# A convolution and attention stack in one loop of slots: another order of the prologue, and other slots for the work behind the loop

## The chip, the cores and the metric

The kernel runs on one core of a Trainium2 chip. The metric is the device time of one execution in microseconds (us). Engines are named as the profile names them: PE is TensorE (PEld its weight loads), DVE is VectorE, ACT is ScalarE, POOL is GpSimd, and SP is SyncE, which issues the DMAs here.

## The reference

The input is x, eight images of 128 channels and 36 x 36 points, all in float32. Two layers are applied, each added to its input.

```python
# layer 0: group norm, 1x1 convolution, attention of all 1296 points over the 34x34 inner ones
x = _conv(_gn(x), w_x) + b_x
q = _conv(x, w_qx, 'SAME'); k = _conv(x, w_kx, 'VALID'); v = _conv(x, w_vx, 'VALID')
a_x = v @ softmax(q^T k)            # the same for a constant image c, which becomes a bias
h = tanh(_conv(concat([x, a_x]), w_h) + b_h)
x = x + _conv(h, w_o) + b_o
# layer 1, on tokens t (8 x 1296 x 128): additive attention, then experts
q = LN(t) @ Wq^T + bq;  k = LN(t) @ Wk^T + bk
scores = sum_d w[d] * tanh(q[i, d] + k[j, d])
t = t + softmax(scores) @ LN(t)
t = t + experts(LN(t))              # 64 experts, each takes its 8 best tokens of an image
```

The scores of layer 1 need a tanh for each pair of points and each of 128 channels. The kernel writes them as a sum of quotients: "features" of queries and keys are exponentials of sums with signs, products of features give a numerator n and a denominator d for groups of terms, and the score is the sum of n / d.

## The kernel before, in words

**Units and slots.** For an image (batch b of 8), the 1296 queries are cut into 3 chunks of 432 and the keys into ten tiles of 128 and a remainder of 16. A chunk with a key tile is a unit; a unit with a full tile has 12 slots, one with the remainder 2, so there are 8 x 3 x (120 + 2) = 2928 slots. `SLOTS` says which rows of which feature block a slot k uses: for k = 0, 1 mod 3 two groups of 32 rows, for k = 2 mod 3 two groups of 64 rows.

**A slot.** `numerators(p)` issues on PE the two products n of slot p (each 432 columns, a PSUM bank each), `denominators(p + 3)` the two products d of the slot three later (`LAG`), followed on ACT by the Ln of both (L898) and, every second slot, one Exp over four (L901), which gives 1 / d. `terms(p)` on DVE multiplies n by 1 / d. In most slots these are two multiplications into rp (L929), which POOL adds up (L936, L938). In the slots of `DVE_PAIRS` = (2, 5, 8, 11) DVE multiplies and adds by itself, four operations (L918 to L925). `sums(u)` joins both totals on POOL, `exps` takes the Exp of the score on ACT (L958).

**Banks.** n products and all background matmuls take their PSUM banks in turn from one pool of four (`ps_n`); d has a pool of two pairs (`ps_d`).

**Work behind the loop.** All other work of layer 0 and layer 1 is written as generators, which are advanced between slots: `normal` (group norm and the 1x1 convolution), `conv_keys`, `layer0`, `tokens`, `keys`, `query_block`, `attend`, `gating`. They stand in four lanes: `first_of_all`, `urgent`, `gates`, `background`. A step says whether the next one has matmuls and how many slots it must rest. Steps without matmuls, most of them emptying a PSUM bank by DVE or ACT, run in `take_turns` ahead of a slot's products; steps with matmuls run in `matmul_turn` behind them, at most one a slot. `balance` allows background matmuls `PACE` columns a slot. `bmm` counts the columns. While the loop works on batch b, the lanes prepare batch b + 1; on the last batch there is none to prepare. Every engine runs its own queue in order, so this order of emission is the order on each engine.

**Convolutions.** A 3x3 convolution works on sums and differences of neighbouring columns (`xwin`, L371 to L375) with "turned" taps: `load_taps` loads three parts of the weight, forms half sums (L308 to L311) on DVE and stores the result in DRAM for later batches. `conv_turns` does four turns of three matmuls each (tile pc) for every group of rows.

**The prologue** is batch 0's share, done before the loop in program order: loads on SP; a matmul chain that makes the constant image's bias hb out of wvc (L218 to L227); `normal(0)`, with statistics at L327; the sign matrix, built on POOL (`signs`, L505); `conv_keys(0)`; `features` (L520 to L552), which multiplies the attention weights by the signs; `layer0(0)`, whose values' and queries' taps are loaded and turned at its start; `tokens(0)`; `keys(0)` for the first three tiles, which are stored in DRAM (kd) and read back (kf) by `prefetch`; three query blocks; and the first three `denominators`.

**After the loop** come the gates of the last batch, the experts and the output.

Of the kernel before, what the change touches and what calls it, by code (L numbers as in the profile page):

```python
# [2 lines left out]

# [41 lines left out]
NF = 8  # L45
# [13 lines left out]
PACE = 365  # L59
# [10 lines left out]
def kernel(  # L70
# [55 lines left out]
    with ExitStack() as loop, ExitStack() as score:  # L126
# [37 lines left out]

        load_x(0)
        wx_s = loaded(w_x, "w_x")
        bx_s = loaded(b_x, "b_x")
        wh_s = loaded(w_h, "w_h")
# [4 lines left out]
        gw_s = loaded(gate_w, "gate_w")  # L173
        gb_s = loaded(gate_b, "gate_b")
# [4 lines left out]
        nc.sync.dma_start(bw_s, bw.to_broadcast([128, 1]))  # L179
        neg_half = const.tile([128, NT], F32, tag="neg_half", name="neg_half")  # L180
# [33 lines left out]

        wvc_s = big_tile("wvc_s")[:, : 9 * C]
        nc.sync.dma_start(wvc_s, w_vc.rearrange("i t o -> i (t o)"))  # L218
        pv = aux("pv")
        for t in range(9):  # L220
            mm(pv[:, :1], wvc_s[:, t * C : (t + 1) * C], c0_s, start=(t == 0), stop=(t == 8))
        vc = small.tile([C, 1], F32, tag="vc", name="vc")
        nc.vector.tensor_copy(vc, pv[:, :1])
        ph = aux("ph")
        mm(ph[:, :1], wh_s[:, 2, :], vc, start=True, stop=True)
        hb = const.tile([C, 1], F32, tag="hb", name="hb")
        nc.vector.tensor_add(hb, ph[:, :1], bh_s)  # L227
# [65 lines left out]
        turned_taps = {}  # L293

        def load_taps(w, name):

            t = big_tile(name)[:, : 12 * C]
            h = t.rearrange("p (y j c) -> p y j c", y=3, j=4)
            if name in turned_taps:
                nc.sync.dma_start(t, turned_taps[name])  # L300
                return h
            g = w.rearrange("i (y x) o -> i y x o", x=3)
            g1 = chunk_tile("g1")[:, : 3 * C].rearrange("p (y c) -> p y c", y=3)
            nc.sync.dma_start(h[:, :, 0, :], g[:, :, 0, :])
            nc.sync.dma_start(h[:, :, 3, :], g[:, :, 2, :])
            nc.sync.dma_start(g1, g[:, :, 1, :])
            half = chunk_tile("half")[:, : 3 * C].rearrange("p (y c) -> p y c", y=3)
            nc.vector.tensor_add(half, h[:, :, 0, :], h[:, :, 3, :])  # L308
            nc.vector.tensor_scalar(half, half, 0.5, None, ALU.mult)
            nc.vector.scalar_tensor_tensor(h[:, :, 1, :], g1, 0.5, half, ALU.mult, ALU.add)  # L310
            nc.vector.scalar_tensor_tensor(h[:, :, 2, :], g1, -0.5, half, ALU.mult, ALU.add)  # L311
            turned_taps[name] = dram.tile([C, 12 * C], F32, tag=name, name=f"{name}_d")
            nc.sync.dma_start(turned_taps[name], t)
            return h
# [3 lines left out]
        def normal(b):  # L318

            if b not in xs:  # L320
                load_x(b)
            r = xs[b][:, :N]
            taps["k"] = load_taps(w_k, "wk_t")
            yield step(4)
            st = small.tile([C, NCH, 6], F32, tag="gn_st", name="gn_st")
            for c in range(NCH):
                nc.vector.bn_stats(st[:, c, :], r[:, c * CH : (c + 1) * CH])  # L327
                yield step()
            mv = small.tile([C, 2], F32, tag="gn_mv", name="gn_mv")
            nc.vector.bn_aggr(mv, st)  # L330
            yield matmuls(1)
            pm = aux("pm")
            bmm(pm[:, :1], gavg, mv[:, 0:1], start=True, stop=True)
            yield TAKE
            gm = small.tile([C, 1], F32, tag="gm", name="gm")
            nc.vector.tensor_copy(gm, pm[:, :1])
            dev = small.tile([C, 1], F32, tag="dev", name="dev")
            nc.vector.tensor_sub(dev, mv[:, 0:1], gm)
            nc.vector.scalar_tensor_tensor(dev, dev, dev, mv[:, 1:2], ALU.mult, ALU.add)
            yield matmuls(1)  # L340
            pv = aux("pgv")
            bmm(pv[:, :1], gavg, dev, start=True, stop=True)
            yield TAKE
            ve = plus_eps(pv[:, :1], 1e-5, [C, 1])
            yield step(2)

            rs = small.tile([C, 1], F32, tag="gn_rs", name="gn_rs")
            rsqrt(rs, ve)
            wxn = chunk_tile("wxn")[:, :C]
            nc.gpsimd.tensor_scalar(wxn, wx_s, rs, None, ALU.mult)  # L350
            yield matmuls(3)
            pb = aux("pb")
            bmm(pb[:, :1], wxn, gm, start=True, stop=True)
            yield TAKE
            bxn = small.tile([C, 1], F32, tag="bxn", name="bxn")
            nc.vector.tensor_sub(bxn, bx_s, pb[:, :1])
            yield matmuls(1)
            for c in range(NCH):
                px = aux("px")
                bmm(px[:, :CH], wxn, r[:, c * CH : (c + 1) * CH], start=True, stop=True)  # L360
                yield TAKE
                nc.vector.tensor_scalar(
                    xpad[:, 1 + c * RC : 1 + (c + 1) * RC, 1 : 1 + W],
                    px[:, :CH].rearrange("p (a b) -> p a b", b=W), bxn, None, ALU.add,
                )

                xe, xo = (xpad[:, 1 + c * RC : 1 + (c + 1) * RC, i::2] for i in range(2))
                u = xwin.rearrange("p j (a b) -> p j a b", b=HW)[:, :, 1 + c * RC : 1 + (c + 1) * RC]
                eng = nc.vector if b == 0 else nc.gpsimd
                e0, e1, o0, o1 = xe[:, :, :HW], xe[:, :, 1:], xo[:, :, :HW], xo[:, :, 1:]  # L370
                eng.tensor_sub(u[:, 0], e0, e1)  # L371
                eng.tensor_add(u[:, 1], o0, e1)
                yield step()
                eng.tensor_sub(u[:, 2], e1, o0)
                eng.tensor_sub(u[:, 3], o1, o0)  # L375
                yield matmuls(1)
# [6 lines left out]
        def conv_keys(b):  # L383
            k = convolved["k"] = big_tile("k0")
            for r0, nr in KROWS:
                yield from conv_turns(
                    taps["k"], (r0, nr), 1, grid(k[:, r0 * WV : (r0 + nr) * WV], WV), True
                )

        def layer0(b):  # L390
# [5 lines left out]
            wv_t = load_taps(w_v, "wv_t")  # L396
            v = big_tile("v0")
            wq_t = load_taps(w_q, "wq_t")
# [112 lines left out]

        def features(sign):
# [4 lines left out]
            feat = []  # L517
            for name, wt in (("a_q", wq1), ("a_k", wk1)):
                wt_s = chunk_tile("w_in")[:, :C]
                nc.sync.dma_start(wt_s, wt)  # L520
                tp = aux("w_t")
                nc.tensor.transpose(tp[:, :C], wt_s, ident)
                wT = chunk_tile("wT")[:, :C]
                nc.vector.tensor_copy(wT, tp[:, :C])
                a = const.tile([C, NF * 128], F32, tag=name, name=name)
                for o in range(0, NF * 128, 512):
                    pa = aux("pa")
                    mm(pa, wT, sign[:, o : o + 512], start=True, stop=True)
                    nc.vector.tensor_copy(a[:, o : o + 512], pa)
                feat.append(a)  # L530
            a_q, a_k = feat
# [3 lines left out]
            nc.vector.tensor_add(wb[:, 1:2], bq_s, bk_s)  # L535
            pcs = aux("pcs")
            for q in range(NF):
                mm(pcs[:, 2 * q : 2 * q + 2], sign[:, q * 128 : (q + 1) * 128], wb,
                   start=True, stop=True)
            cs_s = const.tile([128, NF], F32, tag="cs", name="cs_s")  # L540
# [7 lines left out]
            nc.vector.tensor_tensor(absw, absw, w1_s, ALU.max)  # L548
            psw = aux("psw")
            mm(psw[:, :1], ones, absw, start=True, stop=True)  # L550
            eb_s = const.tile([128, 1], F32, tag="eb", name="eb_s")
            nc.vector.tensor_sub(eb_s, bw_s, psw[:, :1])  # L552
            return a_q, a_k, cs_s, fb_s, eb_s
# [81 lines left out]
        def keys(b, tiles):  # L635
# [3 lines left out]
            for t in tiles:  # L639
                o, n = KT[t]  # L640
                for q0 in (0, NF // 2):
# [6 lines left out]
                    ks = kstp.tile([128, NF // 2, 128], F32, tag="ks", name="ks")  # L648
# [203 lines left out]
        def prefetch(u):  # L852
            if u < len(units):
# [140 lines left out]
        def take_turns(p):  # L994
            for lane in lanes:
                if lane.due(p, False):
                    lane.run(p)

        def matmul_turn(p):
# [3 lines left out]
            for lane in lanes:  # L1003
                while lane.due(p, True) and behind[0] == before:
                    if lane is not first_of_all and balance[0] < 0 or lane is gates and urgent:
                        break
                    lane.run(p)
            balance[0] = min(balance[0] - (behind[0] - before) + PACE, PACE)

        load_x(1)  # L1010
        drain(normal(0))
        sign = signs()
        drain(conv_keys(0))
        a_q, a_k, cs_s, fb_s, eb_s = features(sign)
        drain(layer0(0), tokens(0), keys(0, order[:3]))
# [5 lines left out]
        urgent.append(keys(0, order[3:]))  # L1021
        for u in range(2):
            prefetch(u)
        for p in range(LAG):
            denominators(p)
        pending = deque()
        for p, (u, k) in enumerate(slots):
# [12 lines left out]
            take_turns(p)  # L1040
# [13 lines left out]
            matmul_turn(p)  # L1054
# [6 lines left out]
        take_turns(len(slots))  # L1061
# [185 lines left out]
```

## Time and profile before

| What | us |
|---|---|
| median of 3 runs | 6183.36 (6181.84 to 6194.64) |
| the profiled execution | 6189.61 |
| its span, first to last instruction | 6187.9 |
| prologue, to the first multiplication of the loop | 189.8 |
| loop, to the last one | 5828 |
| after the loop | 170 |

Busy time in the span: PE 5946.4, ACT 5275.0, DVE 4799.7, POOL 4584.2 us. A busy PE is a modelled figure, since matmuls are pipelined. An fp32 matmul of the program appears as two MATMUL records. A wait is written "who <- for whom", with its total, how often and the longest one; a group line gives line, engine, operation, tiles, shapes, number, busy time, mean of one in ns, and the engine's idle time just ahead of it with what ended most of that.

### The profile page before, as it was taken

What the parts mean: (1) busy time and instruction counts of PE and PEld (TensorE: products, weight loads), DVE (VectorE), ACT (ScalarE), POOL (GpSimd) and SP (SyncE); (2) the same over time, 40 slices, a digit from 0 to 9 for tenths busy, and PEclk for the clock granted to TensorE, in tenths of its full rate; (3) what the DMA queues carried; (4) which work ended last, traced back from release to release, by engine and by line L of the source; (5) the groups of instructions that cost most, each with busy time, mean ns of one, the idle gap of its engine ahead of it and who ended that gap; (6) DMA issues with size and microseconds to landing.
All of it is one profiled execution on the core that took longest, in us unless ns stands there. A gap on an engine that the chain in (4) does not pass through costs nothing.

```text
span 6187.9 us, 93159 instructions
## 1 busy us (share of the span) xinstructions
PE 5946.4 (96%) x33576; PEld 2834.5 (46%) x33576; DVE 4799.7 (78%) x9525; ACT 5275.0 (85%) x5371; POOL 4584.2 (74%) x2794
## 2 busy tenths in 40 slices
PE   7999999999999999999999999999999999999996
PEld 5454444544544445444445444454444444544443
DVE  3687778877788787877887777887778878788872
ACT  1798998988989888889988899898998988999980
POOL 3677877777778777778777786877777777787870
PEclk9999999999999999999999999999999999999997
DMA  1210011000110002100111001110011000100017
GB/s 43 70 36 22 21 68 38 33 26 28 67 39 24 26 30 69 37 24 23 50 48 38 22 24 63 41 36 22 21 65 41 31 25 28 63 31 28 25 55 276
DMA packets 150383, 271.40 MB, mean 44 GB/s; under 512 B 45408, under 2 KB 74976, under 8 KB 149920
## 3 DMA queue, kind: packets, MB, share of 16 engines
q1 hardware_dynamic: 149920, 265.44, 12.8%
q8 instruction: 265, 4.34, 0.3%
q14 instruction: 198, 1.62, 0.1%
HBM read 200.94 MB, written 64.19 MB: 43 GB/s over the span
## 4 chain that ended last, share of the span: by engine, by line
PE 65%; DVE 11%; POOL 8%; ACT 8%; issue 8%; DMA 1%; SPq 0%; POOLq 0%; DVEq 0%; ACTq 0%
PE n L875 30%; PE d L875 10%; PE pa L258 7%; ACT lq L898 5%; PE pc L258 5%; DVE n L923 4%; POOL accp L938 4%; DVE rp L929 3%; PE s L258 3%; PE pk L258 3%; DVE accd L925 2%; POOL qf L673 1%; POOL accp L936 1%; PE d L880 1%; PE pq L258 1%
## 5 line engine op out<-in xcount | busy, mean ns | idle before, releaser
L938 POOL TENSOR_TENSOR accp<-accp,rp 128x864 f32<-128x864 f32 x1440 | 2915.1, 2024 | 996.5 <-DVE rp L929 943.5
L875 PE MATMUL n<-qf,kf 32*128 32x432 f32 (+1 forms) x11520 | 3283.6, 574 | 58.9 <-DVE accd L925 19.1
L898 ACT ACTIVATE lq<-d 128x864 f32<-128x864 f32 x2928 | 2517.6, 879 | 555.8 <-PE d L875 498.0
L875 PE MATMUL d<-qf,kf 32*128 32x432 f32 (+1 forms) x11520 | 2907.7, 563 | 46.4 <-ACT lq L898 40.5
L929 DVE TENSOR_TENSOR rp<-n,lq 128x432 f32<-128x432 f32 x3912 | 2160.8, 600 | 557.9 <-PE d L875 398.8
L901 ACT ACTIVATE lq<-lq 128x1728 f32<-128x1728 f32 (+1 forms) x1464 | 2398.2, 1638 | 46.3
L875 PEld LDWEIGHTS n<-qf,kf 32*128 32x128 f32 (+1 forms) x11520 | 1185.9, 185 | 1588.2 <-DVE rp L929 469.1
L875 PEld LDWEIGHTS d<-qf,kf 32*128 32x128 f32 (+1 forms) x11520 | 1046.9, 186 | 449.8 <-issue 241.7
L923 DVE TENSOR_TENSOR n<-n,lq 128x432 f32<-128x432 f32 x1440 | 812.0, 608 | 251.8 <-PE n L875 195.2
L925 DVE TENSOR_TENSOR accd<-n,accd 128x432 f32<-128x432 f32 x1440 | 868.1, 603 | 24.7
L936 POOL TENSOR_TENSOR accp<-rp 128x864 f32<-128x864 f32 x240 | 485.2, 2022 | 244.8 <-DVE rp L929 244.7
L673 POOL TENSOR_SCALAR qf<-qf,cs_s 128x432 f32<-128x432 f32 x192 | 260.7, 1364 | 47.0 <-ACT qf L672 47.0
L258 PEld LDWEIGHTS pa<-xh,e 128*108 128x108 f32 x1920 | 222.1, 174 | 142.9 <-DVE rp L929 63.3
L947 POOL TENSOR_TENSOR accd<-accp,accd 128x432 f32<-128x432 f32 x240 | 265.3, 1106 | 23.3 <-DVE accd L925 3.0
L258 PE MATMUL pa<-xh,e 128*108 128x129 f32 x1920 | 261.3, 283 | 19.9 <-DVE accd L925 13.9
L945 POOL TENSOR_TENSOR accp<-accp 128x432 f32<-128x432 f32 x240 | 264.7, 1103 | 15.8
L258 PE MATMUL s<-q,k 128*116 128x432 f32 x480 | 230.3, 568 | 4.2 <-DVE accd L925 2.7
L444 ACT ACTIVATE e<-s 116x432 f32<-116x432 f32 x240 | 124.8, 520 | 118.7 <-PE s L258 118.4
L258 PEld LDWEIGHTS pk<-xT,a_k 128*128 128x128 f32 x1408 | 171.6, 193 | 105.9 <-DVE n L923 31.8
L435 POOL TENSOR_TENSOR tot<-tot,e 116x432 f32<-116x432 f32 x192 | 212.1, 1105 | 7.3 <-ACT e L444 4.5
L918 DVE TENSOR_TENSOR accd<-n,lq 128x432 f32<-128x432 f32 x240 | 145.1, 604 | 86.7 <-PE n L875 49.7
L258 PE MATMUL pa<-e,vw 116*128 116x432 f32 x480 | 204.6, 549 | 0.0
(208 smaller groups left out, 3870.2 us busy)
## 6 DMA issues: line engine op xcount, KB each, us to landing
kf<-kd SPq DMA_DIRECT2D x240, 512.0 KB
kd<-ks SPq DMA_DIRECT2D x160, 256.0 KB
w<-in_weight_dram SPq DMA_DIRECT2D x32, 1024.0 KB
wk_t<-wk_t_d SPq DMA_DIRECT2D x7, 768.0 KB
wv_t<-wv_t_d SPq DMA_DIRECT2D x7, 768.0 KB
wq_t<-wq_t_d SPq DMA_DIRECT2D x7, 768.0 KB
x<-in_x_dram SPq DMA_DIRECT2D x8, 648.0 KB
t<-tokd SPq DMA_DIRECT2D x96, 54.0 KB
```

The lines of the kernel that those rows point to most:

```text
L258: mm(out, lhsT, rhs, **kw)
L673: nc.gpsimd.tensor_scalar(qf[:, 1, :], qf[:, 0, :], cs_s[:, q : q + 1], None, ALU.mult)
L875: mm(outs[h][:, :CH], kf[rows[h], q, :], qf_of[b, c, q][rows[h], part, :], start=True, stop=True)
L898: nc.scalar.activation(lq[:, o : o + n, :], d[:, :n, :CH], AF.Ln)
L901: nc.scalar.activation(some, some, AF.Exp, scale=-1.0)
L923: mult(ns[h], ns[h], lq[:, o + h, :])
L925: nc.vector.tensor_add(live["d"], ns[h], live["d"])
L929: mult(rp[:, h, :], n, lq[:, o + h, :])
L936: nc.gpsimd.tensor_add(live["p"], live["r"], rp)
L938: nc.gpsimd.tensor_add(live["p"], live["p"], rp)
L945: nc.gpsimd.tensor_add(s[:, 0, :], s[:, 0, :], s[:, 1, :])
L947: nc.gpsimd.tensor_add(d, s[:, 0, :], d)
```

## The change

Loads are issued in another order: x, the 1x1 weight, the raw taps of the keys' convolution, the attention weights, the raw taps of values and queries, then the rest; the load of the second image moves from the prologue to `normal(1)`. Turning the keys' taps moves behind the group norm's variance on DVE (five operations for four); those of values and queries are turned on POOL, ahead of the signs. The chain of the constant image (`context`) and the features become generators, one step of which is taken at each step of `layer0(0)` after the ninth. Before the first denominators only one key tile is computed, straight into its kf buffer; the next two follow the first denominators. In the loop, steps without matmuls are not run in the slots of `DVE_PAIRS`, and steps with matmuls not just ahead of them, save those of the first lane. `PACE` goes from 365 to 400 and the cap on saved columns from `PACE` to twice that.

```diff
-PACE = 365
+PACE = 400
...
+        def load_raw_taps(w, name):
+            h = big_tile(name)[:, : 12 * C].rearrange("p (y j c) -> p y j c", y=3, j=4)
+            g = w.rearrange("i (y x) o -> i y x o", x=3)
+            g1 = chunk_tile("g1")[:, : 3 * C].rearrange("p (y c) -> p y c", y=3)
+            nc.sync.dma_start(h[:, :, 0, :], g[:, :, 0, :])
+            nc.sync.dma_start(h[:, :, 3, :], g[:, :, 2, :])
+            nc.sync.dma_start(g1, g[:, :, 1, :])
+            raw_taps[name] = (h, g1)
+
         load_x(0)
         wx_s = loaded(w_x, "w_x")
         bx_s = loaded(b_x, "b_x")
+        load_raw_taps(w_k, "wk_t")
+        w_in = [loaded(w, "w_in", chunks, "chunk") for w in (wq1, wk1)]
+        load_raw_taps(w_v, "wv_t")
+        load_raw_taps(w_q, "wq_t")
...
+        def context():
+            wvc_s = big_tile("wvc_s")[:, : 9 * C]
+            nc.sync.dma_start(wvc_s, w_vc.rearrange("i t o -> i (t o)"))
+            yield
+            pv = aux("pv")
+            for t in range(9):
+                mm(pv[:, :1], wvc_s[:, t * C : (t + 1) * C], c0_s, start=(t == 0), stop=(t == 8))
+            yield
...
+        def turn_taps(name, eng):
+            h, g1 = raw_taps[name]
+            half = chunk_tile("half")[:, : 3 * C].rearrange("p (y c) -> p y c", y=3)
+            eng.tensor_add(half, h[:, :, 0, :], h[:, :, 3, :])
+            eng.tensor_scalar(half, half, 0.5, None, ALU.mult)
+            eng.tensor_scalar(g1, g1, 0.5, None, ALU.mult)
+            eng.tensor_add(h[:, :, 1, :], half, g1)
+            eng.tensor_sub(h[:, :, 2, :], half, g1)
+            turned_taps[name] = dram.tile([C, 12 * C], F32, tag=name, name=f"{name}_d")
+            nc.sync.dma_start(turned_taps[name], h.rearrange("p y j c -> p (y j c)"))
...
             ve = plus_eps(pv[:, :1], 1e-5, [C, 1])
+            if b == 0:
+                turn_taps("wk_t", nc.vector)
             yield step(2)
...
+                first = (b, t) == (0, order[0])
+                if first:
+                    kf_of[0] = kfp.tile([128, NF, 128], F32, tag="kf", name="kf")
...
-                    ks = kstp.tile([128, NF // 2, 128], F32, tag="ks", name="ks")
+                    if first:
+                        ks = kf_of[0][:, some, :]
+                    else:
+                        ks = kstp.tile([128, NF // 2, 128], F32, tag="ks", name="ks")
...
-        def take_turns(p):
+        def take_turns(p, k):
             for lane in lanes:
-                if lane.due(p, False):
+                if lane.due(p, False) and (k not in DVE_PAIRS or lane is first_of_all):
                     lane.run(p)
 
-        def matmul_turn(p):
+        def matmul_turn(p, k):
             before = behind[0]
             for lane in lanes:
                 while lane.due(p, True) and behind[0] == before:
-                    if lane is not first_of_all and balance[0] < 0 or lane is gates and urgent:
+                    paced = balance[0] < 0 or k + 1 in DVE_PAIRS
+                    if lane is not first_of_all and paced or lane is gates and urgent:
                         break
                     lane.run(p)
-            balance[0] = min(balance[0] - (behind[0] - before) + PACE, PACE)
+            balance[0] = min(balance[0] - (behind[0] - before) + PACE, 2 * PACE)
 
-        load_x(1)
         drain(normal(0))
+        for name in ("wv_t", "wq_t"):
+            turn_taps(name, nc.gpsimd)
         sign = signs()
         drain(conv_keys(0))
-        a_q, a_k, cs_s, fb_s, eb_s = features(sign)
-        drain(layer0(0), tokens(0), keys(0, order[:3]))
+
+        aside = chain(context(), features(sign))
+        for i, _ in enumerate(layer0(0)):
+            if i > 8:
+                next(aside, None)
+        drain(aside)
+        a_q, a_k, cs_s, fb_s, eb_s = (feat[n] for n in ("a_q", "a_k", "cs_s", "fb_s", "eb_s"))
+        drain(tokens(0), keys(0, order[:1]))
         for i, q in enumerate(IN_TURN):
...
-        urgent.append(keys(0, order[3:]))
-        for u in range(2):
-            prefetch(u)
         for p in range(LAG):
             denominators(p)
+        drain(keys(0, order[1:3]))
+        prefetch(1)
+        urgent.append(keys(0, order[3:]))
```

## The prediction, made before the result was known

> **What bounds the kernel.** I read the page first, then stretches of the span, then ScalarE's waits in the loop, then the prologue's timeline. The page's first line, and busy times in one batch in mid-loop against the last third of the last batch (columns: stretch, length, busy us of PE, PEld, DVE, ACT, POOL, granted clock, DMA share, GB/s):
>
> ```profile
> PE 5946.4 (96%) x33576; PEld 2834.5 (46%) x33576; DVE 4799.7 (78%) x9525; ACT 5275.0 (85%) x5371; POOL 4584.2 (74%) x2794
> ```
>
> ```profile
> 3150.00:3890.00 740.00, 723.27 (x4077) 343.85 (x4073) 594.04 (x1179) 656.01 (x668) 569.53 (x346) 0.98 0.11 37
> ...
> 5804.00:6018.00 214.00, 205.08 (x1131) 88.99 (x1126) 177.94 (x345) 198.21 (x190) 167.32 (x93) 0.99 0.07 21
> ```
>
> PE at 98% is modelled and includes time in which it waits with a matmul in its array. A real batch takes 740 us, 247 a chunk; a chunk of the last batch, with next to no work of another batch behind it, takes 214. ScalarE is the engine nearest its limit: 656 of 740, so 84 us idle a batch, 28 a chunk; in the last chunk 16. Next, what ScalarE waits for in the loop (190 to 6018 us; us in total, times, longest), what holds PE over the whole span, and two groups of VectorE's work in slots 2, 5, 8, 11:
>
> ```profile
> ACT lq L898 <- PE d L875: 493.0, 615, 3.3
> ```
>
> ```profile
> PEld n L875 <- DVE rp L929: 469.1, 875, 1.3
> ```
>
> ```profile
> L923 DVE TENSOR_TENSOR n<-n,lq 128x432 f32<-128x432 f32 x1440 | 812.0, 608 | 251.8 <-PE n L875 195.2
> L925 DVE TENSOR_TENSOR accd<-n,accd 128x432 f32<-128x432 f32 x1440 | 868.1, 603 | 24.7
> ```
>
> ScalarE's idle time is nearly all in front of the Ln of a slot, for denominators that PE brings late; PE is held by banks of the numerators that VectorE has not emptied. A slot on VectorE's own account has four operations of 0.6 us where others have two, and its PE products have 64 rows, so two of them fill the array: from the starts of the matmuls, 1.65 us against 0.84. Both engines have their long slot at the same place. The loop is a ring of three nearly full engines (PE, ACT, DVE); what counts is how evenly work falls into slots. The prologue (0 to 190 us) is a chain instead:
>
> ```profile
> 12.30 4.00 PE L221 MATMUL pv<-c,wvc_s 128*128 128x1 f32 x18 [12.30 <-DMA wvc_s<-in_w_vc_dram]
> 16.33 0.16 DVE L223 COPY vc<-pv 128x1 f32<-128x1 f32 x1 [14.29 <-PE pv L221]
> ...
> 19.17 1.62 DVE L327 BATCH_NORM_STATS2 gn_st<-x 128x6 f32<-128x432 f32 x3
> ...
> 28.01 1.82 DVE L372 TENSOR_TENSOR xwin<-xpad 128x216 f32<-128x216 f32 x1
> 29.75 0.37 DVE L374 TENSOR_TENSOR xwin<-xpad 128x216 f32<-128x216 f32 x1
> ...
> 50.40 1.77 PE L528 MATMUL pa<-sign,wT 128*128 128x512 f32 x2 [3.80 <-POOL sign L505]
> ...
> 68.04 0.56 DVE L308 TENSOR_TENSOR half<-wq_t 128x384 f32<-128x384 f32 x1 [5.14 <-DMA wq_t<-in_w_q_dram]
> ...
> 80.22 2.35 PE L258 MATMUL pvw<-w_h,v 128*116 128x128 f32 x20
> ...
> 183.58 1.60 PE L875 MATMUL d<-qf,kf 32*128 32x432 f32 x8 [4.03 <-DMA kf<-kd]
> ```
>
> The statistics of x stand on VectorE behind a copy that waits for the last loaded weight; features (44 to 61 us) and taps (61 to 70) follow one another.
>
> **The prologue, part by part.**
> 1. Order of loading. x moves first in both; the DMA rates of the first 30 us show its 0.66 MB, with the smaller weights, done by 6 us. VectorE's list in the built program now begins with the statistics: they start at about 5.5 instead of 19.17, -13.7. The keys' taps, 0.6 MB at the 300 GB/s seen there, land by 9 us, before anything needs them.
> 2. The keys' taps take five VectorE operations (0.56 x 3 + 0.36 x 2 = 2.4 us; before, four, 2.0, ahead of the statistics). They stand between the variance (23.09) and the bias (25.29), where VectorE waited 2.04 us, and the next operation waits for px until 27.00: hidden. They may delay the two POOL operations of that chain: 0 to 1.2 us, I take 0.8.
> 3. The values' and queries' taps go to POOL, ten operations; nearest rows 1.10 us for a sum and 1.36 for a product with 432 columns, so (3 x 0.98 + 2 x 1.21) x 2 = 10.7 us. The Trainium skill ("SBUF — State Buffer", section "Who interferes with whom") speaks against this: a VectorE operation with two SBUF inputs and a GpSimd one that reads SBUF lock each other out for a whole instruction. The row agrees in kind: an xwin difference takes 0.37 us, and 1.82 beside the sign selects. By the rule each of the twelve could wait a whole POOL operation, some 12 x 1.1 = 13 us; in the trace the twelve lost 3.4 us in all to the selects. Now they run beside the taps instead of the selects: I take the same 3.4, a change of 0, and keep +10 as the bad end.
> 4. The signs (0.95 + 24.8 us) start behind those taps: ready near 11.5 + 10.7 + 25.8, with 1.3 for waits on the lock some 49, as before near 50. The last loaded weight now stands on SP behind the three stores of turned taps, so it is issued near 24 and there by 28; PE wants it at 37. Keys' convolutions end near 44.8 - 12.9 = 32. Values' convolutions follow: eight turns of 1.04 us, context (4.0 + 0.6, now beside other work on VectorE), a transpose and the first features bring PE to 46; the second half of the signs holds it to 49 (0 to 6 us of waiting); then four turns 4.2, features 2.7, sums 2.3, the other transpose: pvw at 59 instead of 80.2. That is -21 including the -12.9. If the signs came first it would be -24; if the lock bites, -11.
> 5. Between 80 and 170 us the instructions and their order are the same: 0.
> 6. Keys. The first tile goes straight into the buffer that the products read, without the trip through DRAM (d waited 4.03 us). d then starts after 16 + 6 matmul records (2.4 + 2.3 us) and an Exp: 5 us after 170.06, instead of 13.5. But the 32 records of two more tiles (4.9 us) now stand in PE's queue between d and the first n; n comes at some 184.3 for 187.87: -3.6. SP: the reload of x(1) moves into the loop, ahead of a kf load, with four slots (8 us) before its use; batches 1 to 6 did so already, at no cost that shows.
>
> Together -25 us (-11 to -32).
>
> **The loop.** The built programs have the same matmuls, VectorE and ScalarE work; only slots change. VectorE's own slots held other work in 23, 32, 30 and 33% (k = 2, 5, 8, 11), now in none; PE had a background turn just ahead of 53, 51, 51 and 50% of them, now of 20, 10, 10, 10% (those of the first lane). Turns move to the places ahead of k = 0 and 1 mod 3, now 65 to 80% filled, before 38 to 61%. PACE and the cap alter no total.
>
> To price it I sorted the idle time of ScalarE in front of each Ln by slot type and by whether background matmuls stood ahead of the last four slots. The loop has 549 us of such idle time. Of the Lns with whole neighbours (391 us), the kinds that become the rule were already in the trace: k = 0 mod 3 after (turn, turn, none, turn), 41 times, 102 ns; k = 1 after (turn, none, turn, turn), 46 times, 4 ns; k = 2 after (none, turn, turn, none), 42 times, 56 ns. Kinds that disappear are dear: k = 2 with a turn right ahead, 306 ns (117 times), 457 (46), 744 (29); k = 0 after (none, turn, turn, turn), 705 (29). With each kind's mean and its number in the new program the 391 us become 122 + 33 + 77 = 232: -159. The reason is in the spacing of d: with the turns behind the long slot and behind the first short one, PE brings denominators every 1.65, 1.75, 1.75 us (a 432-column turn is 0.91), and ScalarE takes 1.62 a slot; with a turn ahead of the long slot one gap is 2.56.
>
> Bounds: sorted only by slot type and the one turn right ahead, the same sum is 440 us against 446, so nothing gained. At the other end every background chunk reaches the last chunk's idle time: 21 x 12 to 14, near -270. As batches 1 to 6 repeat one schedule, 42 cases are only some seven places; I shade -159 to -140. VectorE's short slots get the takes (two of 0.6 beside 1.2): with 1.8, 1.8, 2.2 a triple stays under the 6.0 it takes today, so VectorE is late next, then ScalarE.
>
> **Sum.** Against the profiled execution, 6189.6 us (span 6187.9): -25 - 140 = 6025. The median of the runs, 6183.4, is 6.2 lower: 6018.
>
> **Rivals.**
> - A (0.62): as above, loop -70 to -220: 6018, from 5945 to 6090.
> - B (0.18): the prologue alone. ScalarE's idle time only moves from k = 2 to k = 0, as in the coarse sorting. For it: triples with two turns and two takes took 6.19 us loaded and 6.16 to 6.20 with a clean long slot. Against: those mix turns of 452 and 904 columns. 6183 - 25 = 6158.
> - C (0.14): the takes leaving the long slots free PE's banks as well, which my sorting doesn't see; PE's waits for accd (259.8 us in total) shrink, and the background chunks come near the last ones: 6183 - 25 - 270 = 5888.
> - D (0.06), slower: turns in neighbouring short slots need three of the four banks in a row, so PE stands there, as in slots after four turns in a row: 367 ns at k = 0 and 426 at k = 1 instead of 102 and 4. At the 396 triples with both turns that is +272, so 232 + 272 = 504 against 391: +113 - 25, 6271. It makes the kernel slower once idle time rises by more than 25 us.
> - That the change doesn't do what it says is excluded by the built program's lists.
>
> A measurement tells about 0.2% (12 us) from no change. Faster: A, C and most of B, 0.91; same 0.04 (edges of B and D); slower 0.05. The range runs from 5930 (half of C's extra gain left out) to 6160 (B).
>
> **What would show it.** Right: statistics of x start before 7 us; the second half of the features waits for the signs 0 to 6 us near 46; pvw near 59; first rp near 186 instead of 189.8, 25 us less of everything after it; no other VectorE rows within slots 2, 5, 8, 11; ScalarE's wait of its Ln for d falls from 493 to some 330; a mid-loop batch takes 722 instead of 740. Wrong: twelve xwin operations above 12 us; the batch still at 740 (B) or above (D, with waits of PE for the take's bank in short slots); a new wait of ScalarE's Ln for its buffers.

## The result, and the profile after

The changed kernel takes 6153.51 us (median of 4 runs, 6148.27 to 6159.7) where the kernel before takes 6187.28 (4 runs, 6181.84 to 6194.64) beside it: ratio 0.9937, 95% interval 0.9926 to 0.9949. That is 34 us less, where I had forecast 165 less. In the profiled execution (span 6150.6 us, before 6187.9) I cut time at the first and the last product of the loop on VectorE:

| stretch | before, us | after, us | difference | forecast |
|---|---|---|---|---|
| prologue, to the first rp | 189.8 | 159.8 | -30.0 | -25 |
| loop, first to last product | 5828.3 | 5815.8 | -12.5 | -140 |
| behind the loop | 169.8 | 175.0 | +5.2 | 0 |

The stretch behind the loop has the same instructions in both kernels; it lay between 167.8 and 176.2 us in the 18 profiles kept, with no relation to what was edited. The prologue did what was forecast and a little more; in the 14 other profiles with these same prologue instructions the first rp came between 159.7 and 164.1 us, so its gain is 26 to 30 us. Nearly the whole error lies in the loop.

The page's first line of the changed kernel:

```profile
PE 5963.4 (97%) x33576; PEld 2866.4 (47%) x33576; DVE 4798.4 (78%) x9518; ACT 5281.1 (86%) x5371; POOL 4597.5 (75%) x2804
```

The work is the same; its shares rise only because the span is shorter. One batch in mid-loop, and the last chunk (columns as before):

```profile
3116.00:3852.00 736.00, 725.87 (x4092) 348.48 (x4092) 594.39 (x1180) 660.46 (x671) 572.34 (x346) 1.00 0.12 38
5760.00:5975.00 215.00, 207.27 (x1131) 90.27 (x1131) 179.19 (x348) 199.97 (x193) 168.64 (x94) 0.99 0.08 24
```

A batch takes 736 us instead of 740, not 722. ScalarE is idle for 75.5 us of it, before 84. By the products, the three chunks of batch 2 take 237, 251 and 246 us, where before they took 243, 247 and 248. The waits of the loop (160 to 5976 us; us in total, times, longest):

```profile
PEld n L910 <- DVE rp L964: 584.0, 1039, 1.6
DVE rp L964 <- PE d L910: 539.9, 768, 12.6
ACT lq L933 <- PE d L910: 502.3, 658, 3.3
...
PEld n L910 <- DVE accd L960: 202.1, 478, 1.3
```

Before, the second and the last of these waits were:

```profile
DVE rp L929 <- PE d L875: 398.8, 576, 19.2
PEld n L875 <- DVE accd L925: 259.8, 564, 2.5
```

The third row after is the one that I expected to fall from 493.0 to some 330. It did not fall. The first and the last row show where the time stayed: PE stands less for banks that the long slots (k = 2, 5, 8, 11) hold (accd), and more for banks that the short slots hold (rp: 469.1 before). The same is in VectorE's own groups. The long slot's product lost much of its idle time, which was 251.8 us before, 195.2 of them for PE:

```profile
L958 DVE TENSOR_TENSOR n<-n,lq 128x432 f32<-128x432 f32 x1440 | 815.2, 608 | 138.7 <-PE n L910 83.7
L960 DVE TENSOR_TENSOR accd<-n,accd 128x432 f32<-128x432 f32 x1440 | 867.4, 602 | 24.7
```

The short slots' product took it over. The row before, and the row after:

```profile
L929 DVE TENSOR_TENSOR rp<-n,lq 128x432 f32<-128x432 f32 x3912 | 2160.8, 600 | 557.9 <-PE d L875 398.8
...
L964 DVE TENSOR_TENSOR rp<-n,lq 128x432 f32<-128x432 f32 x3912 | 2174.4, 600 | 739.8 <-PE d L910 539.9
```

So 113 us of idle time left the long slots' product, and 182 arrived at the short slots' one. The order did what it was written to do, and the wait moved with the work.

The prologue, from the timeline (start, us, engine):

```profile
4.83 1.63 DVE L347 BATCH_NORM_STATS2 gn_st<-x 128x6 f32<-128x432 f32 x3 [2.78 <-DMA x<-in_x_dram]
...
10.62 1.36 DVE L324 TENSOR_TENSOR wk_t<-half,g 128x384 f32<-128x384 f32 x1
...
14.22 0.38 DVE L396 TENSOR_TENSOR xwin<-xpad 128x216 f32<-128x216 f32 x1
14.51 1.17 DVE L397 TENSOR_TENSOR xwin<-xpad 128x216 f32<-128x216 f32 x1
...
35.32 2.06 PE L242 MATMUL pv<-c,wvc_s 128*128 128x1 f32 x18
...
47.49 2.08 PE L553 MATMUL pa<-sign,wT 128*128 128x512 f32 x2 [5.68 <-POOL sign L529]
...
57.91 2.31 PE L281 MATMUL pvw<-w_h,v 128*116 128x128 f32 x19
...
152.12 1.01 PE L910 MATMUL d<-qf,kf 32*128 32x432 f32 x8
...
159.83 0.61 DVE L964 TENSOR_TENSOR rp<-n,lq 128x432 f32<-128x432 f32 x1 [12.62 <-PE d L910]
```

The statistics start 14.3 us earlier, pvw 22.3 us earlier, the first rp 30.0 us earlier. One wait grew: PE stands 5.68 us for the signs, where it stood 3.80.

### The profile page after: what moved, and what is told of

It reads as the page before. It is cut to its first block, busy times and chain, and to the rows that moved or that the text cites. A ratio compares the mean times of both kernels' runs of the same rounds, so it can differ in the third digit from the quotient of the medians.

```text
span 6150.6 us, 93223 instructions
## 1 busy us (share of the span) xinstructions
PE 5963.4 (97%) x33576; PEld 2866.4 (47%) x33576; DVE 4798.4 (78%) x9518; ACT 5281.1 (86%) x5371; POOL 4597.5 (75%) x2804
## 3 DMA queue, kind: packets, MB, share of 16 engines
q14 instruction: 198, 1.62, 0.1%
## 4 chain that ended last, share of the span: by engine, by line
PE 76%; ACT 8%; DVE 6%; issue 6%; POOL 2%; DMA 1%; SPq 1%; POOLq 0%; DVEq 0%; ACTq 0%
PE n L910 37%; PE d L910 12%; PE pa L281 7%; ACT lq L933 6%; PE pc L281 5%; PE s L281 3%; PE pk L281 3%; PE pq L281 3%; DVE rp L964 2%; DVE n L958 1%; DVE accd L960 1%; PE d L915 1%; ACT lq L936 1%; PE n L915 1%; ACT e L993 1%
## 5 line engine op out<-in xcount | busy, mean ns | idle before, releaser
L910 PE MATMUL n<-qf,kf 32*128 32x432 f32 (+1 forms) x11520 | 3320.8, 573 | 47.6 <-ACT e L993 13.3
L910 PE MATMUL d<-qf,kf 32*128 32x432 f32 (+1 forms) x11520 | 2983.8, 560 | 39.5 <-ACT lq L933 38.9
L910 PEld LDWEIGHTS n<-qf,kf 32*128 32x128 f32 (+1 forms) x11520 | 1207.1, 184 | 1603.2 <-DVE rp L964 584.0
L910 PEld LDWEIGHTS d<-qf,kf 32*128 32x128 f32 (+1 forms) x11520 | 1088.6, 185 | 420.9 <-issue 225.0
L960 DVE TENSOR_TENSOR accd<-n,accd 128x432 f32<-128x432 f32 x1440 | 867.4, 602 | 24.7
L281 PEld LDWEIGHTS pk<-xT,a_k 128*128 128x128 f32 x1408 | 171.4, 192 | 107.0 <-DVE n L958 33.7
L281 PE MATMUL pk<-xT,a_k 128*128 128x128 f32 (+1 forms) x1408 | 202.6, 287 | 0.1
```

Source lines behind the costliest of these rows:

```text
L281: mm(out, lhsT, rhs, **kw)
L910: mm(outs[h][:, :CH], kf[rows[h], q, :], qf_of[b, c, q][rows[h], part, :], start=True, stop=True)
L960: nc.vector.tensor_add(live["d"], ns[h], live["d"])
```

## The experiments

The theories. **Pattern** is my forecast's: the two bars (takes barred from long slots, turns barred ahead of them) lower ScalarE's wait for d. **Moved wait** is rival B: they only shift it. When the first runs had shown that PACE counts, two more came: **spread** (PACE decides how evenly other batches' work falls into the three chunks of a batch) and **accident** (each setting of PACE and cap gives another schedule, and the one before was a good one). All runs have the changed kernel's prologue, unless a diff shows otherwise. "Loop" is the first to the last product in the profiled execution, as in the table above; the ratio is to the kernel before on the same chip. A loop is of one execution, and executions of one kernel lie up to 21 us apart (12 of them at 380/380: 6176.31 to 6197.37), so loops that differ by less than some 10 us are not told apart here. The texts ahead of the runs name further theories, each with its own forecast.

**The prologue alone.** The loop's rules as before:

```diff
-PACE = 400
+PACE = 365
-                if lane.due(p, False) and (k not in DVE_PAIRS or lane is first_of_all):
+                if lane.due(p, False):
-                    paced = balance[0] < 0 or k + 1 in DVE_PAIRS
+                    paced = balance[0] < 0
-            balance[0] = min(balance[0] - (behind[0] - before) + PACE, 2 * PACE)
+            balance[0] = min(balance[0] - (behind[0] - before) + PACE, PACE)
```

> The changed kernel with the loop's old rules: no slot barred to steps without matmuls, none barred to turns, PACE 365 and cap 365. Theory 'triple' (the three engines even out over about three slots, so where a step stands within three slots costs nothing): the loop is as before, so 6187 - 30 (the prologue as the trace shows it) = 6157, within 10 us of the changed kernel (6153). Theory 'eaten' (placing was worth 140 us and the higher PACE took it back): the same 6157, since both are gone. If the loop's new rules are worth the 12 us seen between the traces: 6157 to 6166 against 6153.

Measured: 6160.28 us, ratio 0.9946 (0.993 to 0.9963); loop 5827.6. Nearly all of the gain is the prologue. What the new loop rules add, all together, is -12 us in the loop of one profile, and the two intervals overlap. All theories had named 6157, so this run doesn't part them.

**The loop's rules apart**, PACE 400 and a cap of 800 in all. No bars at all (the second and third pair of lines above):

> The changed kernel without both bars, PACE 400 and cap 800 kept. Summing for each three slots the largest of PE, ACT and DVE work (durations of the traces) gives 708 us for the second batch against 700 for the kernel before and for the changed one. Theory 'triple': slower than the changed kernel by 8 us in each of 7 batches, 6153 + 56 = 6210. Theory 'eaten': slower by the whole 140 us that the bars save, near 6290. Theory 'nothing in the loop matters': 6157.

Measured: 6227.69 us, 1.0056 (1.0041 to 1.007); loop 5894.9, between the two forecasts that name a cost. Then only the takes barred:

```diff
-                    paced = balance[0] < 0 or k + 1 in DVE_PAIRS
+                    paced = balance[0] < 0
```

> PACE 400, cap 800; only steps without matmuls are barred from VectorE's own slots, matmul turns may stand ahead of them. Theory 'triple': largest-work sum 707 us a batch against 700, so 6153 + 48 = 6201. Theory 'spacing' (a turn ahead of the long slot is what costs): most of the loss of e2 remains, 6200 to 6280. Theory 'banks' (a take in a long slot is what costs): near the changed kernel, 6153 to 6170.

Measured: 6457.97 us, 1.0426 (1.0411 to 1.0442); loop 6122.1. Then only the turns barred:

```diff
-                if lane.due(p, False) and (k not in DVE_PAIRS or lane is first_of_all):
+                if lane.due(p, False):
```

> PACE 400, cap 800; only matmul turns are barred from the place ahead of VectorE's own slots, steps without matmuls may run in them. Theory 'triple': sum 700 us, as the changed kernel: 6153 within 10. Theory 'spacing': the same, 6153 to 6170. Theory 'banks': 6200 or more.

Measured: 6229.34 us, 1.0057 (1.0042 to 1.0072); loop 5890.8. So against the loop without bars at this setting, barring the takes alone costs 227 us, barring the turns alone changes 4, and both together (the changed kernel, 5815.8) gain 79. The parts don't add, and none of the forecasts held for both runs: the takes barred are slower than all three theories had it, and the turns barred stand where only "banks" had put them, which the other run refutes. Nor does the pattern alone set the time. Counted in the built programs (batches 1 to 6), with the turns barred 82, 72 and 12% of the places ahead of k = 0, 1 and 2 mod 3 have a turn and 18% of the long slots have a take; in the changed kernel it is 82, 73 and 12%, and 12%. Nearly one pattern, and 75 us apart. PE's and ScalarE's waits with the takes alone barred, in the loop:

```profile
ACT lq L933 <- PE d L910: 762.5, 827, 4.0
...
PEld n L910 <- DVE accd L960: 392.6, 716, 1.2
DVE n L958 <- PE n L910: 390.7, 393, 3.5
```

In that built program (batches 1 to 6) 65% of the long slots have a turn's matmuls right ahead, and, but for those of the first lane (12%), no take within: the turn's result keeps its PSUM bank through the whole long slot. PE's wait for accd is 392.6 us, against 202.1 with both bars and 248.2 with none. That the held bank is the cause fits these rows; no run tried another bank. And PACE, which I had priced at nothing, costs 67 us between the first two runs (5827.6 to 5894.9).

**PACE and its cap, without bars.** The first two ask whether the pace or the cap of saved columns makes that cost:

> The prologue of the change, the loop without bars, PACE 400 with the old cap of one PACE. With 365 and 365 (e1) it took 6160, with 400 and 800 (e2) 6228. Theory 'triple sums' (largest engine work of each three slots): 704 us a batch against 700, so 6160 + 29 = 6190. Theory 'empty triples' (what costs is that work is done earlier and leaves triples with no turn at all: 12% here, 7% in e1, 17% in e2): 6160 + 68 x 5/9.5 = 6196. If the cap is what costs: 6160; if PACE: 6228.

> The prologue of the change, the loop without bars, the old PACE 365 with the new cap of two PACE. Theory 'triple sums': 706 us a batch against 700, so 6160 + 45 = 6205. Theory 'empty triples' (8% against 7%): 6160 + 5 = 6165. If the cap is what costs: 6228; if PACE: 6160.

Measured: 400/400 takes 6273.71 us, 1.014 (1.0123 to 1.0157), loop 5939.0; 365/730 takes 6232.71, 1.0073 (1.0058 to 1.0088), loop 5895.1. Each of the two alone costs as much as both together, or more; of the forecasts only "the cap costs: 6228" comes near one of them, and it fails at the other. With the bars and a lower pace:

> The changed kernel, both bars, with PACE 380 and cap 760; 370 leaves work undone. Theory 'PACE takes back what the bars give': lower PACE is better, by the slope of e1 to e2 (68 us for 35 columns and the cap) 10 to 40 us, near 6130. Triple sums: 696.5 against 700.4 us a batch, 6154 - 27 = 6127. Empty triples (4% against 5%): 6147. If PACE doesn't matter once the bars are there: 6154.

Measured: 6168.15 us, 0.9966 (0.9953 to 0.9979), loop 5833.0; every forecast had it at 6154 or below. With the bars, a PACE of 370 or 365 leaves the next batch's keys unmade at the place where they are needed, so the setting of the kernel before has no run with them.

Then more settings, to tell a trend from accidents:

> No bars, PACE 380 with a cap of 380; prologue of the changed kernel. Without bars the loop took 5827.6 us at 365/365 and 5939 at 400/400. Theory 'pace': an even spread of the work of other batches is what counts, and 365 is nearly the lowest pace at which that work gets done in time; the loop then grows with PACE, and 380/380 lies between, 5860 to 5900. Theory 'draw': each setting gives another schedule with idle time of its own, and 365/365 is a good one by chance; then 380/380 may come out anywhere from 5830 to 5940, and above 5920 or below 5835 would speak for this.

> No bars, PACE 450 with a cap of 450; prologue of the changed kernel. Theory 'pace': the loop is longer than at 400/400 (5939), 5960 to 6060, with the first chunks of each batch longer and the last shorter. Theory 'draw': a loop below 5930 is as likely as one above, and the three chunks of a batch need not part.

> Both bars, PACE 450 with a cap of 900; prologue of the changed kernel. With bars the loop took 5833 us at 380/760 and 5816 at 400/800. Theory 'pace': with bars 400 is already above what the work needs, so 450/900 is longer, 5840 to 5880, with uneven chunks (the changed kernel: 237, 252, 246). Theory 'bars': the places set the loop and the pace matters little; 5805 to 5830. Theory 'draw': anywhere from 5800 to 5900.

> Both bars, PACE 450 with a cap of 450; prologue of the changed kernel. The three chunks of a batch get 37.5, 40.2 and 34.0 thousand columns of other work, as evenly as in the kernel before (37.0, 40.0, 34.6) and more so than in the changed kernel (35.8, 43.1, 32.8). Theory 'spread': the pace costs what it costs because the chunks become uneven; with an even spread the bars gain on top of the kernel before's loop: 5750 to 5805 us against 5816 of the changed kernel and 5828 of no bars at 365/365, chunks near 245 each. Theory 'accident of the schedule': the spread decides little, 5800 to 5870.

> Both bars, PACE 400 with a cap of 600 instead of 800; 35.8, 42.2 and 33.7 thousand columns by chunk, slightly more even than the changed kernel. Theory 'spread': 5800 to 5816, no worse than the changed kernel. Theory 'accident': off 5816 by more than 15 in either direction.

> No bars, PACE 370 with a cap of 370: 36.0, 41.3 and 34.4 thousand columns by chunk. Theory 'spread': between the loops of 365/365 (5828) and 380/380 (5851), 5828 to 5850. Theory 'accident': as far off as 365/730 was with nearly the same spread (5895), above 5865.

> No bars, PACE 365 with a cap of 500: 36.0, 41.3 and 34.4 thousand columns by chunk, as in the run at 370/370. Theory 'spread': the same time as 370/370 within 10 us. Theory 'cap': a saved balance lets two steps with matmuls follow one another, and that costs; then nearer to 365/730 (5895), 5860 to 5895. Theory 'accident': anywhere.

All settings together, with the columns of other batches' matmuls that fall into a batch's three chunks (thousands, counted in the built programs, batch 3):

| PACE / cap | bars | columns | time, us | ratio (interval) | loop, us |
|---|---|---|---|---|---|
| 365/365 | no | 37.0, 40.0, 34.6 | 6160.28 | 0.9946 (0.993 to 0.9963) | 5827.6 |
| 380/380 | no | 36.0, 42.2, 33.5 | 6181.44 | 0.9984 (0.9976 to 0.9993) | 5851.0 |
| 365/500 | no | 36.0, 41.3, 34.4 | 6202.45 | 1.0025 (1.0015 to 1.0034) | 5865.2 |
| 370/370 | no | 36.0, 41.3, 34.4 | 6200.64 | 1.0018 (1.0011 to 1.0025) | 5868.9 |
| 400/800 | no | 39.2, 45.0, 27.5 | 6227.69 | 1.0056 (1.0041 to 1.007) | 5894.9 |
| 365/730 | no | 36.5, 41.2, 33.9 | 6232.71 | 1.0073 (1.0058 to 1.0088) | 5895.1 |
| 450/450 | no | 41.2, 45.8, 24.7 | 6275.27 | 1.0136 (1.0122 to 1.015) | 5932.6 |
| 400/400 | no | 37.9, 44.6, 29.2 | 6273.71 | 1.014 (1.0123 to 1.0157) | 5939.0 |
| 400/800 | both | 35.8, 43.1, 32.8 | 6153.51 | 0.9937 (0.9926 to 0.9949) | 5815.8 |
| 400/600 | both | 35.8, 42.2, 33.7 | 6154.74 | 0.994 (0.9925 to 0.9955) | 5817.6 |
| 450/450 | both | 37.5, 40.2, 34.0 | 6166.11 | 0.9963 (0.995 to 0.9976) | 5829.7 |
| 380/760 | both | 36.9, 41.6, 33.2 | 6168.15 | 0.9966 (0.9953 to 0.9979) | 5833.0 |
| 450/900 | both | 38.6, 45.2, 27.9 | 6199.35 | 1.0015 (1.0007 to 1.0022) | 5857.9 |

Four things follow. First, **both bars together gain at one setting**: -79 us at 400/800 and -103 at 450/450, the two settings measured both ways; the five loops with bars lie between 5816 and 5858, the eight without between 5828 and 5939. Second, **the setting of the kernel before is the best of the eight without bars**, 23 us ahead of the next, and a step of 5 in PACE costs 41 us. The change gave up that setting, and its bars then bought back about what that cost. Third, **spread explains only the ends**. Where the columns part most (450/450 without bars) the first two chunks take 256 and 264 us and the third 235 instead of some 247 each, and the batch is longer. But the even spread at 450/450 with bars came out at 5829.7 instead of below 5805, which speaks against it; 365/730 and 370/370 have nearly one spread and differ by 26 us, and the two runs with equal columns by chunk agree within 4 us, as it said, but both lie above the 5850 that it allowed. A loop that simply grows with PACE ("pace") missed too, by 9 us at 380/380 and 27 at 450/450, and held at 450/900. "Accident" fits most of the scatter, but it had 400/600 off 5816 by more than 15 us, and that loop took 5817.6; and it is a name, not a cause.

Fourth, **part of these differences goes with the clock that PE is granted**, which no theory had named. Summed over the clock rows of the traces, the loop stands at half speed for 137 us in the kernel before, 65 in the changed one and 137 without bars at 400/800; at 450/450 it is 116 without and 75 with bars, and 164 with the turns alone barred. The executions say the same: a mean granted clock of 0.976 to 0.981 for the kernel before, 0.984 to 0.987 for the changed one, 0.979 to 0.981 without bars at 400/800. The mid-loop batches of 740 and 736 us, shown above, had 0.98 and 1.00; of the prologues, 33 us before and 14 after were at half speed. Among executions of one kernel a lower clock goes with a longer time (before: 6179.61 us at 0.981, 6200.89 at 0.977); a line through 28 of them gives 3 us for 0.001. By that line, as an estimate, some 20 of the 34 us that the change gains go with the clock, more than the loop's own -12, and some 17 and 13 of what the bars gain at 400/800 and 450/450. The clock isn't independent of the schedule. In the changed kernel half-speed stretches begin at 2214.5, 3685.6 and 5156.8 us, each just behind a wait of 3 us in which PE stands ahead of its next d for ScalarE's Ln. Here is the first, with PE's wait, and the clock as the third value from the end:

```profile
2213.61 0.99 PE L910 MATMUL d<-qf,kf 32*128 32x432 f32 x4 [2.97 <-ACT lq L933]
...
2207.70:2214.50 6.80, 3.59 (x16) 0.98 (x13) 3.27 (x6) 6.71 (x7) 3.92 (x2) 1.00 0.00 1
2214.50:2217.90 3.40, 3.40 (x12) 1.02 (x10) 1.78 (x3) 3.37 (x4) 1.37 (x1) 0.50 0.00 0
```

No run holds the clock fixed, so how much of a loop's time it makes stays open, and with it what makes 365/365 good: its loop stood at half speed for 128 us and the one at 365/730 for 126, and they are 67 us apart.

**A prologue without the grown wait.** The queries' taps are turned behind the signs and the last weight is issued ahead of them, at 380/760 with bars:

```diff
-        for name in ("wv_t", "wq_t"):
-            turn_taps(name, nc.gpsimd)
+        turn_taps("wv_t", nc.gpsimd)
         sign = signs()
         drain(conv_keys(0))
         aside = chain(context(), features(sign))
+        next(aside)
+        turn_taps("wq_t", nc.gpsimd)
```

> As e7, and in the prologue the queries' taps are turned on POOL behind the signs instead of ahead of them; the load of the last weight is issued ahead of that turning. In the changed kernel PE waited 5.7 us for the second half of the signs (41.8 to 47.5 us). POOL has 5.9 us less ahead of the signs, so that wait goes: e7 - 5.5. If VectorE's or the taps' wait takes its place (the queries' taps are then ready near 47, wanted near 53): e7 - 0 to 3.

Measured: 6156.74 us, 0.995 (0.9935 to 0.9965), 11.4 less than the same loop without the edit; the loop is the same (5833.3), and the first rp comes at 152.6 us instead of 164.1. In the timeline, the second half of the features now waits next to nothing for the signs, and pvw comes 6.8 us earlier than in the changed kernel:

```profile
42.06 0.30 PEld L553 LDWEIGHTS pa<-sign,wT 128*128 128x128 f32 x2 [0.28 <-POOL sign L529]
42.06 1.12 PE L553 MATMUL pa<-sign,wT 128*128 128x512 f32 x2
...
51.10 2.42 PE L281 MATMUL pvw<-w_h,v 128*116 128x128 f32 x20
```

The same edit with the changed kernel's loop:

> The changed kernel's loop (both bars, PACE 400, cap 800), with its prologue changed in one thing: the queries' taps are turned on POOL behind the signs, and the last loaded weight is issued ahead of them. At PACE 380 this took 11.4 us off the whole and left the loop at 5833.3 for 5833.0. If prologue and loop add up: 6153.5 - 7 to -12 = 6142 to 6147, first term of the loop near 152 to 153 us and a loop of 5816. If the schedule of the loop depends on where it starts, the loop comes out off 5816 by more than 5.

Measured: 6145.97 us (5 runs), 0.9927 (0.9915 to 0.994), loop 5813.8. This is the fastest version measured: 7.5 us under the changed kernel, as forecast, though the two intervals still overlap. The first rp comes at 152.3 us instead of 159.8. That the edit gave 11.4 us there and 7.5 here fits the clock of the two kernels without it: of their prologues, 27 and 14 us were at half speed.

## Why the prediction was wrong, point by point

- **Statistics (step 1).** Forecast 5.5, measured 4.83. Right.
- **The keys' taps (step 2).** Hidden, as said. The last of the five took 1.36 us beside POOL's work, the fourth 0.60. From the variance's end to the scaled weight's it takes 1.62 us for 1.36 before (the first POOL operation 0.83 for 0.57): 0.3 lost, within my 0 to 1.2.
- **Taps on POOL (step 3).** Ten operations took 11.8 us (10.51 to 22.3) for 10.7. The rows were the better guide than the rule that I had cited from the Trainium skill ("SBUF — State Buffer", section "Who interferes with whom"): the twelve xwin operations sum to 7.3 us, 0.38 free and up to 1.18 beside a tap, so they lost 2.8 us, where I took 3.4 and the rule at its worst would have made 13.
- **Signs and pvw (step 4).** A wait of 0 to 6 us near 46 was forecast, I took 3; it is 5.68 us and ends at 47.5. pvw at 57.9 for 59: right, with the wait at its bad end. The run with the signs first shows that it was worth removing.
- **80 to 170 us (step 5).** -1.1 for 0.
- **Keys (step 6).** From xT's products (146.66) to the first rp it takes 13.2 us, before 19.7: -6.6, where I said -3.6. d starts 5.5 us after xT's products, as forecast (5); the first n comes 12.1 us after them, where I had put 14.2: from d to n it takes 6.7 us, before 4.3, and I had added 4.9 for the 32 records of two more tiles. They took 3.84 and delayed n by only 2.4.
- **The loop, first failing step: "PACE and the cap alter no total".** True of totals, and priced at 0. Measured without bars: +67 us for the two together. The price of this schedule was not in its totals. The cost has no row in the profile of the kernel before; it showed when another setting ran.
- **The loop, second failing step: the means of the kinds.** I carried over three kinds of surroundings from 41, 46 and 42 cases, 102, 4 and 56 ns, and forecast -140. In the changed kernel these kinds occur 396, 355 and 438 times and cost 245, 325 and 116 ns: 263 us where I had counted 66. The sum over all Lns with whole neighbours, by k = 0, 1 and 2 mod 3, was 151 + 59 + 181 = 391 us, forecast as 122 + 33 + 77 = 232 and measured as 160 + 166 + 95 = 421: k = 2 fell nearly as far as forecast, k = 1 nearly trebled. I had noted myself that 42 cases are some seven places in a repeated batch. What the sorting left out is how large the turns are: it asked whether a turn stood in a place, not how many columns it had. For k = 1, before, none of the cases had more than 1200 columns in the two nearest turns (as `bmm` counts them). In the changed kernel 156 of the 352 sorted have, and wait 570 ns on average, 89 of the 115 us; the 77 with 1000 to 1200 columns wait 9 ns, and the 119 smaller ones 216. In the four other loops with bars that I sorted, those above 1200 wait 502 to 694 ns and those of 1000 to 1200 wait 10 to 107. So the small mean of the kind came from turns of one size. Size isn't all of it, as the smaller ones show, and no run changes it alone. My other reading, that in a row of like kinds each slot hands its delay to the next, is not borne out: by the number of triples of the same pattern directly ahead (none, one, two, three, more) k = 1 waits 504, 421, 173, 172 and 36 ns.
- **The direction of the bars was right:** -79 and -103 at equal setting, for -140, though some of it goes with the clock, which the forecast hadn't in its sum. So the sum of the loop reads +67 for the setting and -79 for the bars: -12. The other order, bars first, has no run.
- **The rivals.** B has the time (6158 forecast) and half of the cause: idle time moved, though to k = 1, where it had put it at k = 0. The other half, that the setting of the kernel before was itself worth more than its neighbours, was in none, so that B's time came out is in part luck. C is refuted in its size: PE's wait for accd did shrink, by 58 us, and came back as a wait for rp. D, turns in neighbouring short slots, fits the 325 ns at k = 1 and PE's longer wait for rp: the 421 us measured lie between A's 232 and D's 504.

## What to carry to other kernels

Price a change of rules in a schedule by hand in two steps: the rule at a fixed setting, and the setting that the rule forces. Where each setting gives another schedule, measure both rules at several settings; one step of 5 in a pace moved this kernel by more than the whole change did. Don't extrapolate the mean of a kind from a few dozen cases that come from a handful of places, unless they hold the same amounts of work as the cases to come. And compare the granted clock before a difference of a few tenths of a per cent is put down to the order of work.

## What was not expected of the hardware

- A wait of PE in the prologue cost more than itself: the work behind it ran at half the clock. Two matmul records of the features took 2.08 us behind the 5.68 us wait, and 1.12 us in the run with the signs first, where PE had not stood. All 15 profiles with that wait (4.13 to 5.69 us) have a half-speed stretch of 3.4 or 6.8 us that begins between 44.0 and 47.0 us; the two with the signs first have none from 16 to 131 us. The stretches, with the granted clock as the third value from the end, first of the changed kernel:

```profile
47.49:49.57 2.08, 2.08 (x3) 1.05 (x4) 0.00 (x0) 0.00 (x0) 0.00 (x0) 0.50 0.00 0
```

Then of the run with the signs first at 380/760:

```profile
42.06:43.20 1.14, 1.14 (x5) 0.61 (x5) 0.35 (x1) 0.00 (x0) 1.05 (x2) 1.00 0.00 0
```

- VectorE operations stretch beside GpSimd's work, but not each of them: of the twelve xwin operations five were hindered (1.17, 0.48, 1.18, 0.68 and 1.18 us), seven ran in 0.37 to 0.38. It matters what GpSimd does: the four that began within one of its TENSOR_TENSOR operations were all hindered, and of the seven that began within a TENSOR_SCALAR six ran free. The 14 other profiles with this prologue show the same two groups, but for one operation; why is not shown.
- The 18 matmul records of the constant image took 2.06 us between the convolution turns and 4.00 us at 12.3 us of the kernel before. Those of 2.06 us had the full clock. The clock rows of the other trace begin at 30.3 us, so the clock of those of 4.00 us is not on record (a window without rows prints 1.00). But six records of 432 columns that follow them, at 25.11 us, took 0.78 us each, and eight of as many columns at 87.42 us 0.40, so half speed is likely there too.
